# Global attention: the emission order of a period's score tiles and weighted sums, 24 and 8 tiles against 16 and 16

## The chip, the cores and the metric

The kernel runs on one core of one Trainium2 chip. A core has a matrix engine (TensorE, here PE, with its weight loads listed apart as PEld), a vector engine (VectorE, DVE), an activation engine (ScalarE, ACT), a general engine (GpSimd, POOL) and a queue engine (SyncE, SP) that here only issues DMAs. Each runs its own instruction stream in order, and semaphores join the streams. Matmuls write into PSUM, which has eight banks of 128 partitions by 512 fp32 values. The metric is the device time of one execution in microseconds (us), smaller is better. A difference under 0.2% (6.4 us here) can't be told from no change.

## The reference, cut to what matters

The input (2 batches of 2048 tokens, 256 features) is layer-normalized. One branch is a global attention with 16 heads of 16 features. The other is a two-layer network with local attention, whose result gates the first. Only the first branch is touched here.

```python
def _L0_attn_ref(x, W_qkv, W_proj, b_proj, ln_gamma, ln_beta, spatial_centers):
    ...
    attn = jnp.einsum('bhnd,bhmd->bhnm', q, k) * scale
    attn = attn + _spatial_bias(spatial_centers, N, x.dtype)[None, None]
    attn = jax.nn.softmax(attn, axis=-1)
    out = jnp.einsum('bhnm,bhmd->bhnd', attn, v)
    out = jnp.einsum('bnd,ed->bne', out, W_proj) + b_proj
    return out + _layernorm(x, ln_gamma, ln_beta)
...
xn = _layernorm(x, axis=-1)
s = _L0_attn_ref(xn, ...)
g = _silu(_L0_ffn_ref(xn, ...))
x = x + s * g
```

The softmax runs over 2048 keys for each of 2 x 16 x 2048 rows, so the score matrix has 2 x 16 x 2048 x 2048 entries. It never exists as a whole.

## The kernel before, in words

`global_attention` cuts the work into 32 **units**: 2 batches, 4 groups of 4 heads, 4 chunks of 512 queries. The four heads of a group stand on four groups of 32 rows of TensorE (rows 0 to 31 for head 0, and so on), with 16 features and padding in each. So matmuls of four different heads can run beside each other on the array, and two tiles of the same head can't.

The scores are computed twice. The first time only the row maximum is wanted, the second time the exponentials with that maximum subtracted. Three kinds of pieces do it:

- `max_piece(j)` ("P" and the head's number): one score tile of head j, 128 queries by 512 keys, as a matmul of 32 rows into a PSUM bank of ring `p` (L403), and its row maximum by VectorE (`tensor_reduce`, L406). When a unit has all its 64 tiles, the maxima are joined and `augment` sends them through DRAM into a spare row of the queries (`qa`), so that the second score matmul subtracts them. P tiles are 20 rounds ahead of S tiles, so a unit's maxima are ready one whole period before the unit's first S tile.
- `score_piece(j)` ("S"): one tile of head j, 128 keys by 512 queries, as a matmul of 32 rows into a bank of ring `s` (L447), and its exponential by ScalarE into an SBUF tile `e` (L449, 20 buffers). For a unit's first keys GpSimd multiplies some of them by the spatial bias (L453).
- `sum_piece` ("V"): the weighted sum over one tile of 128 keys for all four heads, 128 rows by 32 columns each (L466). Two V in succession share one bank of ring `p` (`po`). Then ScalarE copies it out (L478) and GpSimd adds it to the unit's sum (L479). A V belongs to the key tile that lies LAG = 2 key tiles behind.

Every fp32 matmul is two instructions on TensorE, with a weight load each. A P and an S tile so take two loads and two passes, and the two V in succession 16 of each.

Each ring has four banks, taken in rotation by `bank`. A P tile that takes a bank waits until VectorE has reduced the P tile that had it before. An S tile waits in the same way for ScalarE's exponential. Ring `p` also serves `po` and whatever an X place computes.

Nothing is planned at run time: the order of the instructions is written out by hand in `PATTERN`, and one pass over it is a **period** of four key tiles, that is 16 P, 16 S and 4 V. There are 128 full periods in 32 units. In a period, "N" is a place for small work that is due (`pass_place`, which also counts down the DMA chains that follow a finished unit: row sums out, inverse, fetch, multiply) and for one piece from `aside` (layer norms and transposes of tokens, early loads). "X" is a place for one piece from `others` (a half of the output projection, L578) or from `prep` (query, key and value projections of a later group, L335 and L369). Most X places are empty.

```python
        def bank(name, shape=(P, CH), ring=None):
            ring = ring or other_ring[0]
            turn[ring] += 1
            tags = rings[ring]
            return psr.tile(list(shape), F32, tag=tags[turn[ring] % len(tags)], name=name)
...
            for op in PATTERN:
                if op[0] == "P":
                    max_piece(int(op[1]))
                elif op[0] == "S":
                    score_piece(int(op[1]))
                elif op == "V":
                    sum_piece()
```

Three stretches stand out of this rule. Ahead of the first period, a list of its own (`FIRST`) fills the pipeline. In period 0 the first V V has nothing to sum, so its 32 tiles follow each other. From period 123 on there are no P tiles left, and in the last unit ring `s` has six banks and ring `p` two (`LAST_RINGS`).

Of the kernel before, what the change touches and what calls it, by code (L numbers as in the profile page):

```python
# [17 lines left out]
B, N, D = 2, 2048, 256  # L18
# [62 lines left out]
def spatial_bias(tc, t, pool, tmp, **how):  # L81
# [44 lines left out]

PATTERN = (
    "N P3 S2 P0 S1 S3 P2 S0 P1 X S3 P1 P0 S2 S0 P3 S1 P2 X "  # L130
    "P3 S1 S0 S2 P0 S3 P2 P1 V V N P0 S1 P3 S2 P1 S3 P2 S0 V V"
).split()
SPAN = 4
LEAD = 4
LAG = 2
# [16 lines left out]
def global_attention(tc, t, xA, s_all, s_out, ident, eps_t, x_ch, early):  # L152
# [11 lines left out]
    with ExitStack() as ctx:  # L164
# [474 lines left out]
        for at in range(periods + 1):  # L639
# [8 lines left out]
            after.clear()  # L648
            for op in PATTERN:
                if op[0] == "P":  # L650
# [715 lines left out]
```

## Time and profile before

| what | value |
|---|---|
| three runs | 3178.58, 3179.49, 3183.39 us (median 3179.49) |
| profiled execution, span from first to last instruction | 3181.1 us; the profile tells no other time for it |
| mean granted TensorE clock | 0.990 |
| busy: PE, DVE, ACT, POOL | 3104.0, 2248.9, 2055.1, 1235.4 us |
| first to last V of the global attention | 100.3 to 1776.0 us |
| row maxima (L406), 2048 on DVE | 1260.6 us busy, 683 ns each |
| exponentials (L449), 2048 on ACT | 1052.7 us busy, 604 ns each |
| matmuls of P, S and V (L403, L447, L466), 4096 each | 619, 623 and 600 ns each, overlapping |

"Busy" is the share of time in which an engine had an instruction in flight. For TensorE it says little, since matmuls of different row groups overlap and their ends are modelled. Mean durations include what overlaps with the next instruction of the engine, so the pace of a row of instructions is read from the distance of their starts. A timeline line gives the start and the length in us, then engine, line of the kernel, operation, output and inputs, how many instructions it joins, and in brackets the idle time ahead of it and what ended that.

### The profile page before, as it was taken

What the parts mean: (1) busy time and instruction counts of PE and PEld (TensorE: products, weight loads), DVE (VectorE), ACT (ScalarE), POOL (GpSimd) and SP (SyncE); (2) the same over time, 40 slices, a digit from 0 to 9 for tenths busy, and PEclk for the clock granted to TensorE, in tenths of its full rate; (3) what the DMA queues carried; (4) which work ended last, traced back from release to release, by engine and by line L of the source; (5) the groups of instructions that cost most, each with busy time, mean ns of one, the idle gap of its engine ahead of it and who ended that gap; (6) DMA issues with size and microseconds to landing.
All of it is one profiled execution on the core that took longest, in us unless ns stands there. A gap on an engine that the chain in (4) does not pass through costs nothing.

```text
span 3181.1 us, 58736 instructions
## 1 busy us (share of the span) xinstructions
PE 3104.0 (98%) x22284; PEld 1535.9 (48%) x22284; DVE 2248.9 (71%) x4848; ACT 2055.1 (65%) x4277; POOL 1235.4 (39%) x1096
## 2 busy tenths in 40 slices
PE   8999999999999999999999888999999999999998
PEld 3444444444444444444443455555555555565665
DVE  6898888877777777777774456666666666666653
ACT  4677776677776777777777566556555556666652
POOL 3222223112131221131211455666656665667652
PEclk9999999999999999999999899999999999999999
DMA  3100101000001100000000200000001000000001
GB/s 116 28 13 14 37 10 33 25 8 19 22 22 46 47 14 16 15 22 8 7 8 24 71 10 1 8 1 8 1 1 34 1 20 17 21 21 21 21 21 53
DMA packets 65837, 70.53 MB, mean 22 GB/s; under 512 B 28744, under 2 KB 44188, under 8 KB 65556
## 3 DMA queue, kind: packets, MB, share of 16 engines
q1 hardware_dynamic: 64658, 66.00, 7.2%
q8 instruction: 176, 2.88, 0.4%
q14 instruction: 105, 0.86, 0.1%
q10 hardware_dynamic: 386, 0.52, 0.0%
q0 software_dynamic: 512, 0.26, 0.0%
HBM read 45.26 MB, written 17.53 MB: 20 GB/s over the span
## 4 chain that ended last, share of the span: by engine, by line
PE 82%; DVE 6%; ACT 5%; POOL 3%; issue 3%; DMA 0%; POOLq 0%; SPq 0%; DVEq 0%; ACTq 0%
PE pm L403 20%; PE ps L447 16%; PE po L466 15%; PE pp L855 8%; PE pg L1086 6%; PE po L997 3%; PE py L1125 3%; PE ps L925 3%; ACT sm L946 2%; PE pz L1144 2%; POOL rn L886 1%; PE pw L974 1%; PE px L578 1%; PE pp_wk L335 1%; DVE rs L1059 1%
## 5 line engine op out<-in xcount | busy, mean ns | idle before, releaser
L406 DVE TENSOR_REDUCE mx<-pm 128x1 f32<-128x512 f32 x2048 | 1260.6, 683 | 318.4 <-PE ps L447 304.2
L449 ACT ACTIVATE e<-ps 128x512 f32<-128x512 f32 x2048 | 1052.7, 604 | 193.4 <-PE ps L447 182.4
L403 PE MATMUL pm<-kT,qT 32*128 32x512 f32 x4096 | 1134.5, 619 | 0.1
L447 PE MATMUL ps<-qa,kT 32*128 32x512 f32 x4096 | 1091.8, 623 | 0.7 <-ACT e L449 0.7
L479 POOL TENSOR_TENSOR o<-o,part 128x512 f32<-128x512 f32 x217 | 274.9, 1267 | 1268.3 <-ACT part L478 1256.6
L403 PEld LDWEIGHTS pm<-kT,qT 32*128 32x128 f32 x4096 | 480.9, 183 | 358.9 <-DVE mx L406 240.8
L447 PEld LDWEIGHTS ps<-qa,kT 32*128 32x128 f32 x4096 | 438.3, 183 | 222.1 <-ACT e L449 179.2
L466 PE MATMUL po<-e,v 128*32 128x512 f32 x4096 | 494.2, 600 | 1.9 <-DVE mx L406 1.9
L960 POOL TENSOR_TENSOR sm<-sm,wls 128x512 f32<-128x512 f32 (+1 forms) x224 | 236.6, 1086 | 403.1 <-DVE wls L952 402.6
L855 PE MATMUL pp<-weights,xA 128*128 128x512 f32 x768 | 358.5, 615 | 1.5 <-DVE s L583 0.8
L1086 PE MATMUL pg<-hc,weights 128*128 128x512 f32 x640 | 284.3, 592 | 0.0
L478 ACT COPY part<-po 128x512 f32<-128x512 f32 x217 | 127.1, 586 | 242.6 <-PE po L466 240.3
L466 PEld LDWEIGHTS po<-e,v 128*32 128x32 f32 x4096 | 107.7, 109 | 350.2 <-DVE mx L406 174.5
L946 ACT ACTIVATE sm<-sm,wmx 128x256 f32<-128x256 f32 (+1 forms) x512 | 249.3, 488 | 7.0 <-DVE wmx L938 6.3
L855 PEld LDWEIGHTS pp<-weights,xA 128*128 128x128 f32 x768 | 142.7, 193 | 166.0 <-issue 161.5
L886 POOL TENSOR_TENSOR rn<-rn,mhalf 128x8 f32<-128x8 f32 x128 | 211.1, 1649 | 13.8 <-DVE rn L885 12.2
L1086 PEld LDWEIGHTS pg<-hc,weights 128*128 128x128 f32 x640 | 121.1, 190 | 150.2 <-issue 139.4
L876 ACT ACTIVATE sqq<-pp 128x512 f32<-128x512 f32 x128 | 76.3, 596 | 178.7 <-DVE swp L874 168.0
L938 DVE CUSTOM_DVE_ANT_0 sm<-ps,mask 128x256 f32<-128x256 f32 (+1 forms) x512 | 176.2, 408 | 2.4 <-PE ps L925 2.3
L877 POOL TENSOR_TENSOR rot<-rot,swp 128x512 f32<-128x512 f32 x128 | 160.6, 1269 | 34.0 <-DVE swp L874 33.6
L1095 DVE SCALAR_TENSOR_TENSOR u<-pg,vecs,gl 128x512 f32<-128x512 f32 x80 | 60.0, 750 | 150.5 <-ACT gl L1091 76.2
L925 PE MATMUL ps<-xT,xT 64*128 64x128 f32 x1984 | 132.3, 281 | 6.9 <-DVE xT L903 6.9
(172 smaller groups left out, 3303.1 us busy)
## 6 DMA issues: line engine op xcount, KB each, us to landing
s<-in_x_dram SPq DMA_DIRECT2D x8, 512.0 KB
qk_wk<-stage_wk SPq DMA_DIRECT2D x16, 256.0 KB
kT<-qk_wk SPq DMA_DIRECT2D x128, 32.0 KB
qk_wq<-stage_wq SPq DMA_DIRECT2D x16, 256.0 KB
qT<-qk_wq SPq DMA_DIRECT2D x128, 32.0 KB
qa<-qk_wq SPq DMA_DIRECT2D x128, 32.0 KB
s_out<-s SPq DMA_DIRECT2D x8, 512.0 KB
s<-s_out SPq DMA_DIRECT2D x16, 256.0 KB
```

The source lines that it names most:

```text
L403: nc.tensor.matmul(ps, qT[rows, q0 : q0 + P], kT[rows, c * CH : (c + 1) * CH], start=True, stop=True)
L406: nc.vector.tensor_reduce(mxs[n][:, j * TPC + i, c : c + 1], ps, AX.X, ALU.max)
L447: nc.tensor.matmul(ps, kT[rows, kt * P : (kt + 1) * P], qas[n % 2][rows, :], start=True, stop=True)
L449: nc.scalar.activation(e, ps, AF.Exp)
L466: nc.tensor.matmul(pos[n][j * HP : (j + 1) * HP, :], v[:, kt, (r + j) * VW : (r + j) * VW + HP], es.pop((n, kt, j)), start=(kt % 2 == 0), ...
L479: nc.gpsimd.tensor_add(os[n], os[n], part)
L855: nc.tensor.matmul(ps, xA[b][:, k, at : at + P], W["qkv"][:, k, n * INNER : (n + 1) * INNER], start=(k == 0), stop=(k == 1),)
L886: nc.gpsimd.tensor_tensor(rn, rn, mhalf, ALU.pow)
L925: nc.tensor.matmul(pss[r][:, x, pa * P : (pa + 1) * P], S["qT"][rows, 2 * hb + x, :], kvs[l, b, kt, "k"][rows, 2 * hb + x, :], start=True, ...
L946: nc.scalar.activation(sm[:, x, lo:], sm[:, x, lo:], AF.Exp, scale=-1.0, bias=mx[:, hb, r, x : x + 1], accum_out=ls[:, hb, r, x : x + 1],)
L960: nc.gpsimd.tensor_mul(sm, sm, ls[:, hb, r, :, None].to_broadcast([P, 2, 2 * P - lo]))
L1086: nc.tensor.matmul(ps[:mw], W["1"][:, k, at : at + mw], hc[:, k, :], start=(k == 0), stop=(k == 1))
```

## The change

The order within a period is written anew. Before, a period is 24 tiles (12 P, 12 S), two V, 8 tiles (4 P, 4 S), two V, with an N at the start and one ahead of the 8 tiles, and an X after the 8th and after the 16th of the 24. The four groups of eight tiles have four different orders of the heads. After it, a period is twice the same half: N, 8 tiles, X, 8 tiles, two V. All groups of eight have the order of the first one of before, in which the heads come round every four tiles (3 2 0 1 3 2 0 1). The numbers of N, P, S, X and V in a period, the lead of P over S and the lag of V are the same, and no instruction is added or removed.

```diff
-PATTERN = (
-    "N P3 S2 P0 S1 S3 P2 S0 P1 X S3 P1 P0 S2 S0 P3 S1 P2 X "
-    "P3 S1 S0 S2 P0 S3 P2 P1 V V N P0 S1 P3 S2 P1 S3 P2 S0 V V"
-).split()
+TILES = "P3 S2 P0 S1 S3 P2 S0 P1"
+PATTERN = " ".join(["N", TILES, "X", TILES, "V V"] * 2).split()
```

## The prediction

> **What bounds the kernel now.** I read the page first, for the engines and the chain that ended last.
>
> ```profile
> span 3181.1 us, 58736 instructions
> PE 3104.0 (98%) x22284; PEld 1535.9 (48%) x22284; DVE 2248.9 (71%) x4848; ACT 2055.1 (65%) x4277; POOL 1235.4 (39%) x1096
> ...
> PE 82%; DVE 6%; ACT 5%; POOL 3%; issue 3%; DMA 0%; POOLq 0%; SPq 0%; DVEq 0%; ACTq 0%
> ```
>
> TensorE carries the chain, but its busy time hides waits, since row groups overlap. So I went to the timelines of one period in the middle, with no X work, engine by engine. VectorE:
>
> ```profile
> 806.26 2.48 DVE L406 TENSOR_REDUCE mx<-pm 128x1 f32<-128x512 f32 x4 [1.52 <-PE ps L447]
> 810.04 7.32 DVE L406 TENSOR_REDUCE mx<-pm 128x1 f32<-128x512 f32 x12 [1.30 <-PE ps L447]
> ```
>
> The 12 maxima of the long block run back to back: (7.32 - 0.68) / 11 = 0.60 us from start to start. VectorE idles only at a block's start, 1.30 and 1.52 us. The weight loads show who is held by it:
>
> ```profile
> 808.88 0.18 PEld L403 LDWEIGHTS pm<-kT,qT 32*128 32x128 f32 x1 [0.84 <-DVE mx L406]
> ...
> 811.39 0.18 PEld L403 LDWEIGHTS pm<-kT,qT 32*128 32x128 f32 x1 [0.30 <-DVE mx L406]
> ...
> 811.99 0.29 PEld L403 LDWEIGHTS pm<-kT,qT 32*128 32x128 f32 x2
> ...
> 812.58 0.29 PEld L403 LDWEIGHTS pm<-kT,qT 32*128 32x128 f32 x2
> 813.18 0.18 PEld L403 LDWEIGHTS pm<-kT,qT 32*128 32x128 f32 x1 [0.30 <-DVE mx L406]
> ...
> 814.98 0.29 PEld L403 LDWEIGHTS pm<-kT,qT 32*128 32x128 f32 x3
> 816.02 0.16 PEld L466 LDWEIGHTS po<-e,v 128*32 128x32 f32 x8 [0.76 <-DVE mx L406]
> ```
>
> From 811.39 a P tile's load comes every 0.60 us, as VectorE gives a bank back: P6, P7, P8, P9. The last of the 12 loads at 814.98, and the sums follow 1.05 us later, when it has run through. The TensorE timeline gives the sums themselves:
>
> ```profile
> 816.03 1.92 PE L466 MATMUL po<-e,v 128*32 128x512 f32 x16
> 817.88 0.69 PE L403 MATMUL pm<-kT,qT 32*128 32x512 f32 x1
> ```
>
> So from the start of two V to the next tile it is 1.85 us. Finally the windows from sum to sum (length first, then busy times), the short one and the long one:
>
> ```profile
> 816.03:819.81 3.78, 3.78 (x34) 1.26 (x33) 2.10 (x5) 1.73 (x4) 1.01 (x1) 1.00 0.02 4
> 819.81:828.80 8.99, 8.99 (x68) 4.09 (x64) 8.13 (x15) 7.64 (x16) 2.75 (x3) 1.00 0.01 2
> ```
>
> A period is 3.78 + 8.99 = 12.77 us. Less 1.85 for each pair of V, the 8-tile block takes 1.93 and the 24-tile block 7.14. The clock is 1.00 in both.
>
> **The change, part by part.** No instruction is added or removed: the pieces of a period only stand in another order. What counts is what the first, the second and the third eight tiles of a block cost.
>
> *First eight.* The ring is free, so nothing waits: 1.93 us, as in the 8-tile block. VectorE's first maximum starts 1.16 us after the block (808.88 to 810.04), the time a first tile needs to come through.
>
> *Second eight.* P5 to P8 need the banks of P1 to P4. The first eight of the long block stand in the very order that both new halves start with, so its rows can be used directly. The fourth maximum starts at 810.04 + 3 x 0.60 = 811.84 and ends at 812.52; P8's load is the row at 812.58. If the V come next, they start 1.05 us later, at 813.63. The 16-tile block is then 813.63 - 808.88 = 4.75 us, and the second eight cost 4.75 - 1.93 = 2.82.
>
> *Third eight.* They cost 7.14 - 4.75 = 2.39, four maxima at 0.60 us: the pipe is full and only VectorE's pace counts. So the second eight of a block pay 0.43 us more than the third, because they also pay VectorE's late start. The change takes a third eight away (-2.39) and adds a second eight to the short block (+2.82): **+0.43 us a period**, 2 x (4.75 + 1.85) = 13.20 against 12.77. Seen from VectorE: four maxima fewer lie under the first pair of V and four more under the second, but it ends its eighth at 810.04 + 7 x 0.60 + 0.68 = 814.92, while the next first tile comes through at 813.63 + 1.85 + 1.16 = 816.64. It idles 1.72 us twice, 3.44 in place of 2.82.
>
> *Rotation of the heads.* With heads coming round every four tiles, a tile finds its row group free: P8 (head 1) follows S6 (head 1, loaded at about 811.39), whose two passes need about 0.97 us. Before, the later eights have the same head twice within two tiles (P0 S2 S0; S1 P2, P3 S1), and the third has three S in succession, with ScalarE idle 0.22 us in the middle. A P load there comes at 814.06, 0.28 us behind VectorE's pace (813.18 + 0.60). But VectorE did not stop for it, and P12's load at 814.98 again comes right behind the eighth maximum (810.04 + 7 x 0.60 + 0.68 = 814.92). So of a gain between 0 and 0.28 us a period I take 0. A loss would need a tile in the new second eight that ends behind P8; the latest other is S8 (head 0), free to start when P6 leaves the rows at about 812.4, and through 0.97 us later, at 813.4.
>
> *N places.* The N places stand 6.60 us apart, where now it is 8.99 and 3.78 in turn. Their VectorE work is at most two pairs of statistics (1.2 us), and the idle 1.72 us of either block hides it, better than the 1.30 of now. The DMA chains behind `pass_place` count places: row sums to inverse is two places, a full period, 13.20 in place of 12.77; inverse to fetch one place, 6.60 in place of 3.78; SP's waits grow by nothing. `augment` still has a whole period. All cost 0; if the inverse came late, VectorE would stand, at 0.24 us for the reciprocal plus the wait, 32 times at most.
>
> *Buffers.* 20 `e` tiles now live at the end of a long block, 16 after the change: no wait is added. `po` needs the bank of P5, whose maximum ends at 813.12, before the V at 813.63. The copy out of `po` (ACT, 0.58 us) finds ScalarE idle: its eight exponentials need about 4 us from 810.09 and the V end at 815.5. Without that margin of about 1.3 us the next P4 would wait.
>
> *GpSimd.* In a unit's first period 12 multiplications by the bias (0.73 us) race the second pair of V, which now comes at 4.75 + 1.85 + 4.75 = 11.35 into the period with eight of them needed, against 10.92 now. The intervals of those eight periods show stalls of 0.07 us, once 1.39 and once 0.24: a gain of 0 to 2 us, I take 2.
>
> *X places.* A projection period shows the second eight with X work on both sides:
>
> ```profile
> 403.09 1.11 PE L578 MATMUL px<-wp,oc 128*128 128x256 f32 x4
> 404.13 0.69 PE L447 MATMUL ps<-qa,kT 32*128 32x512 f32 x1
> ...
> 406.48 1.13 PE L578 MATMUL px<-wp,oc 128*128 128x256 f32 x4
> ...
> 409.52 1.92 PE L466 MATMUL po<-e,v 128*32 128x512 f32 x16
> ```
>
> The block starts at 401.14 and ends at 409.52 (8.38 us); up to where the second X stands, 5.34 us. Two halves of that are 10.68 against 8.38 + 1.93 = 10.31: +0.37. In a period with two projections of queries, keys or values, eight tiles after an X run at 1.93 to 1.95 us wherever they stand (535.34, X at 537.27 and 541.13, V at 544.98): 2 x 5.79 against 9.64 + 1.93, so +0.01.
>
> *Sum.* Periods 1 to 122 have both kinds of tiles. By what the timeline has between the sums, 12 of them have preparations, 13 projections, 97 neither (or a transpose at N, the same on both sides): 97 x 0.43 + 13 x 0.37 + 12 x 0.01 = 41.7 + 4.8 + 0.1 = 46.6. Period 0 has 32 tiles in a row either way: 0. Periods 123 to 127 have S alone. The first, with four banks, has halves bounded by four exponentials, 1.2 + 4 x 0.49 + 1.05 = 4.2, twice, against 7.1: +1.3. The other four, with six banks, 1.2 + 2 x 0.49 + 1.05 = 3.2 twice against 5.30 + 1.07: almost nothing, at most 0.2 each. Together +2, which cancels GpSimd's -2. The sum is +46.6, 3181.1 + 46.6 = 3227.7 for the profiled execution. It lies 1.6 us above the median of the three runs, 0.05%, so I forecast **3179.5 + 46.6 = 3226.1 us**.
>
> A rule of the Trainium skill speaks for another sum. "TensorEngine Tiling (Array Packing)", section "Theoretical Speedup", gives up to four times the speed where the contraction is 32 rows or less. By it alone any eight tiles would cost the same wherever they stand, and the change would be worth 0. The rows of this case, 1.93, 2.82 and 2.39 for the three eights, decide against it; the same page's section "PSUM Bottleneck" says why: emptying PSUM doesn't get faster with the array.
>
> **The rivals.** *Neutral or a little faster: the rotation counts.* If the second eight cost under 2.60 us (a 16-tile block under 4.53), the new period is shorter than the old. For it: ScalarE's 12 exponentials take from 810.09 to 816.44, 6.35 us, where 12 x 0.49 + 0.11 = 5.99 would do, so the old order wastes up to 0.36 us a long block. If all that lay on the path and both halves had it back, a period would be 0.43 - 2 x 0.36 = -0.29: 122 x -0.29 = -35 us, 3144. If half: about 0.07 x 122 = +9, 3188. Against it: P8's load is tied to the fourth maximum, in a stretch that already has the new order. 5% together.
>
> *No effect*: the second eight cost as the third, 2.39, the bank wait hidden under TensorE's own 1.93 us. Then 3180. Against it is the measured 0.60 between loads from 811.39 on. 2%.
>
> *Slower still: a new wait at the V.* ScalarE's last exponential or the copy out of `po` holds a bank in each half. One exponential's pace, 0.49 us, a period is 122 x 0.49 = 60 us on top: 3286. Against it stands the margin of 1.3 us. A small one (0.1 us in either half) gives 24 us: 3250. 7% together.
>
> **How the numbers follow.** The forecast has 86%, and its own range is +-0.06 us on each half (the reading of 4.75, where releases lie 0.05 us behind the ends) times 2 x 122, about +-14 us: 3212 to 3240. It holds a little over 8 in 10, so the range needs no other case. By the cases above faster by over 0.2% (6.4 us, what a measurement can tell) has 3%, within that 3%, slower 94%.
>
> **What would show it.** Right: sum to sum 6.60 us twice in a plain period, VectorE with eight maxima in a row and about 1.7 us idle ahead of each, the P8 load 3.70 us after a block's start, and nothing changed behind 1780 us but the shift. Wrong: a block other than 4.75 us, or a wait at the loads of L466 or L447 that is named for ScalarE or GpSimd.

## The result, and the profile after

The changed kernel takes 3225.26 us (median of four runs, 3222.91 to 3232.15) against 3180.33 us (four runs, 3178.58 to 3183.39): the ratio is 1.0145 with a 95% interval of 1.0130 to 1.0159. It is 44.9 us slower. The forecast was 3226.1 us, 46.6 us slower.

The profiled execution has a span of 3230.4 us against 3181.1. The windows say where the 49.3 us lie. Ahead of each window's busy times stands its length. First the stretch from the first to the last pair of V in the kernel before, and what follows it:

```profile
100.33:1774.66 1674.33, 1671.19 (x12397) 701.31 (x12397) 1306.53 (x2263) 1203.47 (x2306) 367.27 (x341) 1.00 0.08 20
1774.66:3181.10 1406.44, 1344.37 (x9441) 790.53 (x9440) 869.51 (x2429) 808.79 (x1890) 834.76 (x691) 0.98 0.06 19
```

and the same in the changed kernel:

```profile
103.56:1820.56 1717.00, 1715.28 (x12398) 767.62 (x12397) 1295.87 (x2263) 1197.59 (x2307) 367.54 (x342) 1.00 0.08 20
1820.56:3230.40 1409.84, 1347.09 (x9441) 792.07 (x9440) 869.82 (x2429) 809.06 (x1890) 835.32 (x691) 0.98 0.06 18
```

The periods cost 42.7 us more. The stretch behind them, in which no instruction changed, is 3.4 us longer in this execution, and the start 3.2 us, with a granted clock of 0.96 in the first 89.4 us where it was 1.00. Both look like this execution's own: another kernel with the even split, `split16_old_rotations` below, reaches its first pair of V at 100.18 us and takes 1406.0 us behind the last one, as the kernel before does.

One plain period (one without X work) of the changed kernel, from sum to sum, as windows (813.32 and 819.92 are the starts of two pairs of V):

```profile
813.32:819.92 6.60, 6.60 (x49) 3.03 (x48) 4.88 (x9) 4.66 (x11) 0.00 (x0) 1.00 0.08 17
819.92:826.53 6.61, 6.61 (x49) 2.99 (x49) 5.04 (x10) 4.67 (x11) 1.27 (x1) 1.00 0.19 45
```

The two intervals are 6.60 and 6.61 us, where they were 8.99 and 3.78. TensorE's weight loads in the first of them:

```profile
815.18 0.18 PEld L401 LDWEIGHTS pm<-kT,qT 32*128 32x128 f32 x1 [0.84 <-DVE mx L404]
...
817.08 0.18 PEld L401 LDWEIGHTS pm<-kT,qT 32*128 32x128 f32 x1 [0.73 <-DVE mx L404]
...
817.68 0.18 PEld L401 LDWEIGHTS pm<-kT,qT 32*128 32x128 f32 x1 [0.30 <-DVE mx L404]
...
818.28 0.29 PEld L401 LDWEIGHTS pm<-kT,qT 32*128 32x128 f32 x2
...
818.87 0.29 PEld L401 LDWEIGHTS pm<-kT,qT 32*128 32x128 f32 x2
819.92 0.16 PEld L464 LDWEIGHTS po<-e,v 128*32 128x32 f32 x8 [0.76 <-DVE mx L404]
```

P5 to P8, counted from the block's start (in an order such as P3 S2 the number names the head), load at 817.08, 817.68, 818.28 and 818.87, each behind one more maximum. P8 stands 3.69 us behind the block's start, and the sums follow 1.05 us later: a block of 4.74 us. VectorE in the same period, and ScalarE in its first half:

```profile
816.34 4.88 DVE L404 TENSOR_REDUCE mx<-pm 128x1 f32<-128x512 f32 x8 [1.73 <-PE ps L445]
821.13 0.24 DVE L522 RECIPROCAL rsum<-rsum 128x16 f32<-128x16 f32 x1
822.94 4.28 DVE L404 TENSOR_REDUCE mx<-pm 128x1 f32<-128x512 f32 x7 [1.57 <-PE ps L445]
...
816.38 4.08 ACT L447 ACTIVATE e<-ps 128x512 f32<-128x512 f32 x8 [0.47 <-PE ps L445]
```

Eight maxima run back to back, and VectorE idles 1.73 us ahead of them (1.57 where a reciprocal lies in the gap). The third row counts seven because the view ends at 826.6; a row that a view cuts off counts only what it holds, here and below. ScalarE's eight exponentials start with the maxima and end 0.76 us earlier (820.46 against 821.22), so ScalarE gives its banks back ahead of VectorE. Waits at the loads of S tiles that are named for ScalarE come to 15.6 us in the whole changed kernel, where they were 179.9.

### The profile page after: what moved, and what is told of

It is laid out like the page before. It is cut to its first block, busy times and chain, and to the rows that moved or that the text cites. A ratio compares the mean times of both kernels' runs of the same rounds, so it can differ in the third digit from the quotient of the medians.

```text
span 3230.4 us, 58607 instructions
## 1 busy us (share of the span) xinstructions
PE 3154.1 (98%) x22284; PEld 1604.5 (50%) x22284; DVE 2239.3 (69%) x4848; ACT 2049.4 (63%) x4277; POOL 1236.4 (38%) x1096
## 4 chain that ended last, share of the span: by engine, by line
PE 82%; DVE 6%; ACT 5%; POOL 3%; issue 3%; DMA 1%; POOLq 0%; SPq 0%; ACTq 0%; DVEq 0%
PE pm L401 24%; PE po L464 15%; PE ps L445 13%; PE pp L853 8%; PE pg L1084 5%; PE po L995 3%; PE py L1123 3%; PE ps L923 3%; ACT sm L944 2%; PE pz L1142 2%; POOL rn L884 1%; PE pw L972 1%; PE px L576 1%; PE pp_wk L333 1%; DVE rs L1057 1%
## 5 line engine op out<-in xcount | busy, mean ns | idle before, releaser
L401 PE MATMUL pm<-kT,qT 32*128 32x512 f32 x4096 | 1182.3, 626 | 0.6 <-DVE mx L404 0.5
L445 PE MATMUL ps<-qa,kT 32*128 32x512 f32 x4096 | 1111.6, 617 | 0.7 <-ACT e L447 0.7
L401 PEld LDWEIGHTS pm<-kT,qT 32*128 32x128 f32 x4096 | 492.3, 183 | 466.7 <-DVE mx L404 347.4
L445 PEld LDWEIGHTS ps<-qa,kT 32*128 32x128 f32 x4096 | 466.9, 183 | 94.0 <-issue 66.2
L464 PE MATMUL po<-e,v 128*32 128x512 f32 x4096 | 494.1, 600 | 0.0
L464 PEld LDWEIGHTS po<-e,v 128*32 128x32 f32 x4096 | 107.1, 109 | 347.7 <-DVE mx L404 173.7
```

The lines of the kernel that those rows point to most:

```text
L401: nc.tensor.matmul(ps, qT[rows, q0 : q0 + P], kT[rows, c * CH : (c + 1) * CH], start=True, stop=True)
L445: nc.tensor.matmul(ps, kT[rows, kt * P : (kt + 1) * P], qas[n % 2][rows, :], start=True, stop=True)
L464: nc.tensor.matmul(pos[n][j * HP : (j + 1) * HP, :], v[:, kt, (r + j) * VW : (r + j) * VW + HP], es.pop((n, kt, j)), start=(kt % 2 == 0), ...
```

## The experiments

Two theories were to be told apart, and each part of the edit taken alone. Edits are cut to the lines that matter; a new PATTERN that stands without an old one takes the place of the changed kernel's. "Even split" means 16 and 16 tiles. The bank theory is the prediction's: a block's time follows from the maxima that free its banks; the second eight tiles pay for VectorE's late start and the third don't. Its rivals: the order of the heads has a price of its own, the loss grows in step with the tiles moved, or TensorE pays for being stopped and restarted whatever VectorE does.

### The order of the heads alone

```diff
-    "N P3 S2 P0 S1 S3 P2 S0 P1 X S3 P1 P0 S2 S0 P3 S1 P2 X "
-    "P3 S1 S0 S2 P0 S3 P2 P1 V V N P0 S1 P3 S2 P1 S3 P2 S0 V V"
+TILES = "P3 S2 P0 S1 S3 P2 S0 P1"
+PATTERN = " ".join(["N", TILES, "X", TILES, "X", TILES, "V V N", TILES, "V V"]).split()
```

> The old split, 24 tiles, two V, 8 tiles, two V, with the single order of heads in all four groups of eight. Bank theory (the time of a block is set by the maxima that free its banks, the order of the heads is worth nothing): the last P of the long block still loads behind the eighth maximum, so 7.14 and 1.93 us for the two blocks, 12.78 us a period, 3180 us in all, within 6 us of the kernel before. Rotation theory (the order of the heads has a price of its own that the change also moved): up to 0.28 us less in each long block, 122 x 0.28 = 34 us, 3146 us; or, if the single order costs something, slower than before by part of the 45 us that were lost.

3180.88 us against 3178.29; ratio 1.0006 (0.9997 to 1.0015). In the split of before the order is worth nothing that can be measured.

### The split alone, with the old orders

```diff
-    "N P3 S2 P0 S1 S3 P2 S0 P1 X S3 P1 P0 S2 S0 P3 S1 P2 X "
-    "P3 S1 S0 S2 P0 S3 P2 P1 V V N P0 S1 P3 S2 P1 S3 P2 S0 V V"
+    "N P3 S2 P0 S1 S3 P2 S0 P1 X S3 P1 P0 S2 S0 P3 S1 P2 V V "
+    "N P3 S1 S0 S2 P0 S3 P2 P1 X P0 S1 P3 S2 P1 S3 P2 S0 V V"
```

> The new split, 16 and 16, with the four old orders of heads, one for each group of eight. Bank theory: the same 6.60 us from sum to sum as the changed kernel, 3225 us within 6 us. Rotation theory: if the single order has a price, this kernel gets it back (under 3215); if the old orders have one, it is above 3235, since in each second eight a head comes twice within two tiles.

3258.12 us against 3178.29; ratio 1.0250 (1.0236 to 1.0264). Against the kernel before, the even split with one order stood at 1.0145, so the old orders cost it 0.0105 x 3178.29 = 33 us more, and here the bank theory as written missed. The order has a price, as the rotation theory said, but not in the second eight, where that theory put it: the first half, with an old order in its second eight, has its 6.60 us as in the changed kernel. The trace shows the place. A plain period has sums 6.60 and 6.88 us apart, and VectorE's timeline differs in the second half alone:

```profile
772.15 4.88 DVE L406 TENSOR_REDUCE mx<-pm 128x1 f32<-128x512 f32 x8 [1.73 <-PE ps L447]
776.95 0.24 DVE L524 RECIPROCAL rsum<-rsum 128x16 f32<-128x16 f32 x1
778.76 0.69 DVE L406 TENSOR_REDUCE mx<-pm 128x1 f32<-128x512 f32 x1 [1.57 <-PE ps L447]
779.63 3.68 DVE L406 TENSOR_REDUCE mx<-pm 128x1 f32<-128x512 f32 x6 [0.18 <-PE pm L403]
```

The second half begins with P3 S1 S0 S2 P0: one P among the first four tiles, and the second P on the rows that S0 has just taken. After its first maximum VectorE waits 0.18 us for the second tile, and the second maximum starts 0.87 us behind the first in place of 0.60: all that follow are 0.27 late, and so is the block, 0.28 us. The order counts where it decides when the first maxima can start, in the first eight tiles of a block that has a second eight. In the old split that group stood third in its block, where VectorE had tiles waiting, and there the order cost nothing, as the first experiment shows.

### A split half way between

```diff
+A, B4 = "P3 S2 P0 S1", "S3 P2 S0 P1"
+PATTERN = " ".join(["N", A, B4, "X", A, B4, "X", A, "V V N", B4, A, B4, "V V"]).split()
```

> A split half way between the two: 20 tiles, two V, 12 tiles, two V, with heads coming round every four tiles. Bank theory: the last P of the 20 waits for the sixth maximum, 1.16 + 0.68 + 5 x 0.60 + 0.06 = 4.90 us, plus 1.05 = 5.95; that of the 12 for the second, 1.16 + 0.68 + 0.60 + 0.06 = 2.50, plus 1.05 = 3.55. With two pairs of V (3.71) that is 13.21 us a period, the same as 16 and 16: 3225 us, within 8. What counts is only whether the short block holds over four P. Balance theory (the loss grows in step with the tiles moved to the short block): half of it, +0.21 us a period, 3203 us.

3243.03 us against 3178.29; ratio 1.0206 (1.0191 to 1.0222). The plain periods do as the bank theory says: the sums are 7.80 and 5.45 us apart, together 13.25 against 13.21 forecast, no half-way price. The total is above the forecast since the X places now split the 20 tiles into 8, 8 and 4: a period with two preparations takes 16.1 us against 15.3 in the even split, one with two projections 14.8, where the even split pays 0.60 in each half that has one, 14.4 in all. That was left out of the expectation. The balance theory (3203) falls.

### The bank wait taken away by shorter reads

Two pairs of kernels, each with the split 24 and 8 and the split 16 and 16 in the single order of heads. VectorE and ScalarE read a half or a quarter of each tile, and each V reads that part two or four times, so TensorE does the same matmuls; the rest of the keys and queries is left out, and the result is another one. GpSimd's multiplication is fitted to the part (128 columns in the quarter-read kernels).

```diff
-            nc.vector.tensor_reduce(mxs[n][:, j * TPC + i, c : c + 1], ps, AX.X, ALU.max)
+            nc.vector.tensor_reduce(mxs[n][:, j * TPC + i, c : c + 1], ps[:, : CH // 2], AX.X, ALU.max)
...
-            nc.scalar.activation(e, ps, AF.Exp)
+            nc.scalar.activation(e[:, : CH // 2], ps[:, : CH // 2], AF.Exp)
...
-                    es.pop((n, kt, j)),
+                    es.pop((n, kt, j))[:, None, : CH // 2].to_broadcast([P, 2, CH // 2]),
```

> Split 24 and 8 with the single order of heads; each maximum and each exponential reads only 256 of a tile's 512 columns, and each V reads that half of the exponentials twice (so the result is that of half the keys and queries, and not the reference's); TensorE's work is the same. Bank theory: VectorE's pace falls from 0.60 to about 0.34 us and ScalarE's from 0.49 to about 0.28 (by the distance of 0.26 and 0.21 us between 512- and 256-column rows of the same engines), the banks come back before TensorE wants them, and every eight tiles cost 1.93. A plain period is then 4 x 1.93 + 3.71 = 11.43 us, -1.35 against 12.78: 97 x -1.35 + 13 x -0.5 - 2 = -139, 3041 us, within 15. Rival (the split itself costs, by drains and restarts of TensorE): this kernel falls by as much, and the difference to the other half-read kernel stays at 0.43 us a period.

> The same with half of each tile read (so the result is again not the reference's), with the split 16 and 16 of the changed kernel. Bank theory: with no bank wait the second eight cost 1.93 like the third, two blocks of 3.86 and two pairs of V, 11.43 us a plain period; equal to the other half-read kernel within 6 us, 3041. Rival (the split itself costs): 0.43 us a period more than the other, 97 x 0.43 = 42 us, about 3083.

3015.01 and 3043.06 us against 3180.75; ratios 0.9483 (0.9467 to 0.9499) and 0.9570 (0.9555 to 0.9584). The difference is 28 us: not 0, as the bank theory said, and not 42. From sum to sum it is 7.49 and 3.78 us in one kernel and 5.77 twice in the other, so 11.27 and 11.55 a period. Less 1.85 for the V, the three eights of a block cost 1.93, 1.99 and 1.72. Here is why the second still pays, from the weight loads and VectorE in the first of the two:

```profile
771.98 0.18 PEld L401 LDWEIGHTS pm<-kT,qT 32*128 32x128 f32 x1 [0.47 <-DVE mx L404]
771.98 0.18 PEld L445 LDWEIGHTS ps<-qa,kT 32*128 32x128 f32 x1
772.16 0.18 PEld L401 LDWEIGHTS pm<-kT,qT 32*128 32x128 f32 x1
772.17 0.18 PEld L445 LDWEIGHTS ps<-qa,kT 32*128 32x128 f32 x1
772.31 0.18 PEld L401 LDWEIGHTS pm<-kT,qT 32*128 32x128 f32 x1
```

```profile
771.50 1.65 DVE L404 TENSOR_REDUCE mx<-pm 128x1 f32<-128x256 f32 x4 [2.13 <-PE ps L445]
```

The first maximum takes 0.43 us and starts 1.16 us behind the block (770.34), however short it is. P5 still loads in time, but P6 (772.31) waits for the second maximum, 0.14 us beyond the moment at which the rows come free (772.17, where the S tile beside it loads). Its first pass then takes 0.53 us (772.31 to 772.84) where P5's takes 0.43, and the two together are 0.24 of the 0.27 us by which the second eight exceed the third. Half the read was not enough to take the wait away. A quarter should be, if the theory holds:

```diff
-ps[:, : CH // 2]
+ps[:, : CH // 4]
...
-                    es.pop((n, kt, j))[:, None, : CH // 2].to_broadcast([P, 2, CH // 2]),
+                    es.pop((n, kt, j))[:, None, : CH // 4].to_broadcast([P, 4, CH // 4]),
```

> As the half-read kernel with split 24 and 8, but each maximum and each exponential reads 128 of a tile's 512 columns, and each V reads them four times (so the result is not the reference's). In the half-read pair the third eight cost 1.72 us and the second still 1.99, because the second P of the second eight was released by the second maximum 0.14 us after its row group was free and its first pass then took 0.53 in place of 0.43 us. Bank theory: with maxima about 0.12 us shorter that wait is gone as well, the second and third eight both cost 1.72, and a plain period is 1.93 + 1.72 + 1.72 + 1.93 + 3.71 = 11.01 us, 0.26 less than with half a tile: 3015 - 97 x 0.26 = 2990 us. Rival (what is left in the half-read pair is a price of the split itself): the same for this kernel.

> The same with a quarter of each tile read (the result again not the reference's), with the split 16 and 16. Bank theory: 2 x (1.93 + 1.72) + 3.71 = 11.01 us a plain period, equal to the other quarter-read kernel within 6 us, 2990. Rival (a price of the split itself): the 0.28 us a period that the half-read pair still differs by stays, 97 x 0.28 = 27 us, 3017.

2986.56 and 2991.86 us against 3181.24; ratios 0.9385 (0.9371 to 0.9399) and 0.9404 (0.9388 to 0.9420). The pairs of V in plain periods, first with 24 and 8, then with 16 and 16:

```profile
720.74 1.92 PE L464 MATMUL po<-e,v 128*32 128x512 f32 x16
727.97 1.92 PE L464 MATMUL po<-e,v 128*32 128x512 f32 x16
731.75 1.92 PE L464 MATMUL po<-e,v 128*32 128x512 f32 x16
```

```profile
721.09 1.92 PE L464 MATMUL po<-e,v 128*32 128x512 f32 x16
726.60 1.92 PE L464 MATMUL po<-e,v 128*32 128x512 f32 x16
732.11 1.93 PE L464 MATMUL po<-e,v 128*32 128x512 f32 x16
```

A period is 7.23 + 3.78 = 11.01 us in the one and 5.51 + 5.51 = 11.02 in the other. Without the bank wait the split costs nothing. The 5.3 us between the two medians lie elsewhere: of the 5.8 us between the two spans, 4.3 are in the stretch behind the attention (1405.23 and 1409.57 us), which varies by itself. With a whole, a half and a quarter of each tile read, the even split costs 0.43, 0.28 and 0.01 us a period, and TensorE stops and restarts as often in all three. A price of stopping TensorE, as the rival had it, is out. Both engines' reads were shortened at once, so the pairs alone don't tell VectorE's maxima from ScalarE's exponentials; that the maxima hold the loads is read from the rows of the changed kernel above.

The Trainium skill's page "TensorEngine Tiling (Array Packing)", section "PSUM Bottleneck", says that tiling speeds up the array and not the emptying of PSUM. The three pairs agree: at a quarter read, eight tiles behind the first eight cost 1.72 or 1.73 us in either split, at a whole read 2.82 and 2.39.

### No second eight at all

```diff
+TILES = "P3 S2 P0 S1 S3 P2 S0 P1"
+PATTERN = " ".join(["N", TILES, "X V", TILES, "V"] * 2).split()
...
-            if kt % 2 == 0:
-                pos[n] = bank(f"po_{n}_{kt}", ring="p")
+            pos[n] = bank(f"po_{n}_{kt}", ring="p")
...
-                    start=(kt % 2 == 0), stop=(kt % 2 == 1),
+                    start=True, stop=True,
...
-            if kt == 1:
+            if kt == 0:
```

> No second eight at all: 8 tiles, one V, four times a period, with each V in a bank of its own (start and stop in every one), copied out and added alone, so four copies by ScalarE and four additions by GpSimd a period in place of two. Bank theory: a block of eight has no bank wait, 1.93 us, and one V from its start to the next tile is half of 1.71 + 0.145, 1.00 us; 4 x 2.93 = 11.72 us a plain period against 12.78. X work then stands ahead of a V, with no bank wait to hide in, about 1.04 us for a projection and 1.92 for a preparation. 97 x -1.06 + 13 x -0.22 + 12 x +0.29 = -102: 3078 us. Rival (the copies are the next bound: the fourth P of a block waits for the copy of the last V, which stands behind four exponentials on ScalarE): up to 0.3 us in each block, 4 x 0.3 x 122 = 146, no gain at all, 3180 to 3225 us.

3162.23 us against 3178.29; ratio 0.9948 (0.9934 to 0.9962): faster than both kernels, but only 16 us of the 102 came. Two things eat the rest. A plain period takes 12.02 us, not 11.72: every second block is 3.09 us in place of 2.93, since five pieces a block now take banks of a ring of four, and the second P of such a block loads 0.16 us late, behind the third maximum of the block before. (Behind the 40th period projections cost 1.1 us each and preparations 1.9 to 2.0, about as expected.) And the first 40 periods are slow, 569.8 us together against 540.5 in the kernel before, while periods 41 to 127 take 1079.3 against 1130.0: most of 1 to 33 take 12.4 to 14.5 us, and 34 to 40, with preparations, 16.0 to 20.1. Their layer-norm pieces on VectorE used to lie under the second of two V, and a single V is too short:

```profile
131.45 0.38 DVE L251 BATCH_NORM_STATS2 st<-s 128x6 f32<-128x256 f32 x1
131.87 0.18 DVE L252 BATCH_NORM_AGGREGATE mvs<-st 128x2 f32<-128x6 f32 x1
131.97 0.39 DVE L251 BATCH_NORM_STATS2 st<-s 128x6 f32<-128x256 f32 x1
132.40 0.18 DVE L252 BATCH_NORM_AGGREGATE mvs<-st 128x2 f32<-128x6 f32 x1
132.50 2.45 DVE L404 TENSOR_REDUCE mx<-pm 128x1 f32<-128x512 f32 x4
...
144.70 1.44 DVE L322 SCALAR_TENSOR_TENSOR s<-s,rss,bet 128x256 f32<-128x256 f32 x1
```

The maxima start right behind the statistics, with no idle time ahead of them: VectorE is the late one. The last row shows a part of it that is easily overlooked. L322 takes 0.48 us by itself (L324 in the kernel before: 29 times of 32), but 1.3 to 1.5 us in 27 of its 32 here, each of which overlaps a GpSimd instruction by 1.0 to 1.2 us. All 32 are 25.8 us longer than 0.48 each; how much of that reached the end isn't shown. So the order was chosen for each period, four eights where no X work and no side work is left and 24 and 8 in the single order elsewhere:

```diff
+PATTERN = " ".join(["N", TILES, "X", TILES, "X", TILES, "V V N", TILES, "V V"]).split()
+EIGHTS = " ".join(["N", TILES, "V", TILES, "V"] * 2).split()
...
-            if kt % 2 == 0:
+            first, last = alone[0] or kt % 2 == 0, alone[0] or kt % 2 == 1
+            if first:
                 pos[n] = bank(f"po_{n}_{kt}", ring="p")
...
-                    start=(kt % 2 == 0), stop=(kt % 2 == 1),
+                    start=first, stop=last,
...
-            for op in PATTERN:
+            alone[0] = not (aside or prep or others)
+            for op in EIGHTS if alone[0] else PATTERN:
```

> The order is chosen for each period: four blocks of eight with one V each where nothing is due at the X places and no piece of side work is left when the period begins, and 24 and 8 with the single order of heads elsewhere. By the traces, 64 periods behind the 40th are plain, at 12.02 us (measured with four eights everywhere) in place of 12.78, 64 x -0.76 = -49, and the last five periods, S alone, 8.7 in place of 10.1, -6: 3178 - 55 = 3123 us, within 10. Rival (part of what the four eights lost lies in the plain periods too, by the copies or by the second P that waits for a bank): 3145 or more.

3127.11 us against 3180.75; ratio 0.9834 (0.9819 to 0.9849), 53.6 us faster than the kernel before and some 98 faster than the changed one. In its plain periods the V come every three us:

```profile
812.12 1.07 PE L467 MATMUL po<-e,v 128*32 128x512 f32 x8
815.05 1.06 PE L467 MATMUL po<-e,v 128*32 128x512 f32 x8
818.13 1.06 PE L467 MATMUL po<-e,v 128*32 128x512 f32 x8
821.06 1.07 PE L467 MATMUL po<-e,v 128*32 128x512 f32 x8
```

## Why the prediction was right, point by point

**The second eight.** P8's load was forecast 3.70 us behind the block's start and came 3.69 behind; the block was forecast at 4.75 and is 4.74. The period was to be 13.20 and is 13.21, 0.43 above the one before. This one term is nearly all of the result, and it was read off rows of before that already had the bank state of the new block. Their first eight, whose maxima release P5 to P8, also had the new order. Their second eight, in which P5 to P8 stand, did not (S3 P1 P0 S2 S0 P3 S1 P2), so the argument that this stretch "already has the new order" holds for its first half alone. It did no harm: `split16_old_rotations` has that very second eight in its first half and takes the same 6.60 us. The read-length pairs show the cause, not only the size.

**VectorE's idle time.** Forecast 1.72 us ahead of each row of maxima; it is 1.73, and 1.57 with a reciprocal in the gap.

**Rotation at 0.** Right for what was asked: with the split of before the single order changes the time by 0.06%, inside its interval. The bounds of the prediction treated the order as a matter of row groups in the third eight. What the runs showed in its place is another role: with the old orders the even split loses 80 us (3258.12 - 3178.29) in place of 45, because its second block would start with one P among four tiles. So the new order was worth some 33 us to the new split, which the prediction's sum held without saying so, as it took its rows from the first group of eight.

**N places, buffers, `po` and its copy.** No wait of these kinds lengthens a plain period, as forecast. The loads of L464 do name GpSimd 15 times (8.2 us in all, in the eight periods with multiplications by the bias), but with the same 0.76 and 0.30 us that such loads have elsewhere, and the intervals there are 6.60 or 6.61. The N places were even a small gain, where the forecast had 0: before, VectorE's side work made periods 3, 7 and 31 0.13, 1.15 and 0.14 us longer than the others, and `split24_one_rotation` repeats all three. With the even split none of the three has such a delay.

**X places.** Thirteen periods with projections were to lose 0.37 us each and twelve with preparations 0.01. In the trace after, work for X comes in the second half of a period and in the first of the next, 0.60 us in each half. Periods 1 to 122 without preparations are together 43.7 us longer, against 41.7 + 4.8 - 2 = 44.5. The twelve with preparations are 1.3 us shorter in all, not 0.1 longer. Most of that is work that moved: in periods 35 and 67 a projection took the place of one of two preparations, which went to periods 36 and 68, so 35 and 67 are 0.45 and 0.43 us shorter and 36 and 68 0.77 and 0.78 longer. Period 39 is 0.26 shorter; the other nine differ by at most 0.04.

**GpSimd.** The second intervals of the units' first periods, late before by 0.24, 1.39 and five times 0.07 us, 1.98 in all, are 6.60 or 6.61 us after: the gain of 2 us is there. For the 1.39 the rows speak for another cause than the forecast's race with the multiplications. These ended at 518.45, and GpSimd's addition, which the trace names, at 519.67, a full us before the pair of V at 520.71. VectorE's L324, beside GpSimd's work, lasted 2.06 us in place of 0.48, so the block's first maximum ran only from 519.88 to 520.56, and the V need its bank.

**The last periods.** Forecast +2 us; periods 123 to 127 take 55.6 against 54.4, +1.2. The parts were off both ways: +0.17 for the first, forecast at +1.3, and +0.08 to 0.31 for the other four, forecast at almost nothing, at most 0.2.

Together 43.7 - 1.3 + 1.2 = 43.6 us in periods 1 to 127 against a forecast of 46.6. The pair of V behind them comes 0.9 us sooner, which the forecast had not, and that makes the 42.7 of the windows. The medians have 44.9, and their interval, 1.0130 to 1.0159, covers 41 to 51 us and with it all three numbers. So that the total came within 2 us of the medians is partly luck; that the plain period came within 0.01 us is not. The neutral rival needed a 16-tile block under 4.53 us and had a stretch of 4.74; the slower rival needed a wait at a V that isn't there.

## What to carry to other kernels

Where an engine fills a small ring of buffers and another empties it, a block that fits in the ring waits for nothing, and the block that first exceeds it pays for the emptying engine's start as well as its pace; evening out two blocks so that both exceed the ring makes both pay. Look for the row that is released by the first emptying, and price the block by it and not by the mean. Work that hides under a pause loses its cover when the pause is cut in two, so a faster order may be right only for the periods that have no such work.

## What the runs showed of the hardware that was not expected

- A block's first maximum starts 1.16 us behind the block's first load at a whole, a half and a quarter read (815.18 to 816.34, 770.34 to 771.50, 722.60 to 723.76), so its bank comes free 1.16 us plus its own length behind the start. The 1.16 us are what a first fp32 tile of 512 columns with 32 rows took to come through when four row groups started together.
- Eight tiles of two passes cost TensorE 1.72 us when the stream isn't interrupted, as at a quarter read (four passes of 0.43 on each row group), and 1.93 as the first of a block. A pass that follows a wait is longer in the trace than one that streams, 0.53 us to the next pass on its rows (818.28 to 818.81 in the changed kernel) against 0.43 (822.32 to 822.75).
- The stretch behind the attention, with the same instructions in all kernels, took 1405.2 to 1409.8 us in the eleven profiled executions, and the first 89 us once had a clock of 0.96. So up to 4.6 us behind the attention, and some 3 ahead of it, can be an execution's own.
- VectorE's L324 (L322 after the change), an operation on 128x256 values that takes 0.48 or 0.49 us, took 1.57 to 2.06 us in the three places of the kernel before where a GpSimd instruction overlapped it by 1.25 us or more, and 1.3 to 1.5 us in 27 of 32 places with four eights. Overlaps of up to 0.33 us left it at 0.48. No run takes GpSimd's work away, so that GpSimd is the cause is read from these overlaps alone.
